# Rows backwards as the last scan direction, and outputs and inputs of a joint stage handed out to the same end

## The chip, the cores and the metric

The kernel runs on one core of one Trainium2 chip. A core has a matrix engine (TensorE, PE), a vector engine (VectorE, DVE), an activation engine (ScalarE, ACT), a general-purpose engine (GpSimd, POOL) and a sync engine (SyncE, SP) that here issues every transfer. The engines run side by side, each in the order of its own instructions, and wait for one another by semaphores. The metric is the time of one execution on the device, in microseconds (us); less is better.

## The reference

Four images of 64 x 64 positions and 96 channels go through four layers. The first two are selective scans in four directions, the last two are attention without a softmax, followed by a feed-forward network with quantised numbers. What matters here is a scan layer (`DI` = 192 inner channels, 16 states):

```python
xz = einsum('bhwc,ec->bhwe', group_norm(x), in_proj_w)      # 96 -> 2 x 192
xc, z = split(xz)
xc = silu(depthwise_conv3x3(xc) + conv_b)
xs = [xc by rows, xc by columns, rows backwards, columns backwards]   # k = 0, 1, 2, 3
dts, B, C = split(einsum('bkdl,kcd->bkcl', xs, x_proj_weight))
delta = softplus(einsum('bkrl,kdr->bkdl', dts, dt_projs_weight) + bias)
# for each direction, channel and state, along the 4096 positions l:
h[l] = exp(delta[l] * A) * h[l-1] + delta[l] * xs[l] * B[l]
ys[l] = sum over states of h[l] * C[l]  + D * xs[l]
y = ys of the four directions, each put back to its positions, added
y = layernorm(y) * silu(z)
x = x + einsum('bhwd,cd->bhwc', y, out_proj_w)
```

The four directions are added, so the order in which they are computed is free.

## The kernel before, in words

**Units.** A unit is one scan layer on one pair of images; there are four, in the order (layer 0, pair 0), (layer 0, pair 1), (layer 1, pair 0), (layer 1, pair 1). The 192 channels of two images are 384 rows: three tiles of 128, of which the third (j = 2) holds the last 64 channels of both images. Before a unit's scan stand its inputs (`scan_inputs`): normalisation, projection, convolution, silu; after it its outputs (`scan_outputs`): layer norm, gate, projection, residual. After the last unit come the token layers 2 and 3 (`token_layers`).

**The scan (`PairScan`, lines 370-733).** `steps` (line 374) lists 48 steps: four directions k, four chunks ci of 1024 positions, three tiles j. In each step the 16 states are taken two at a time: ScalarE makes the exponentials, ScalarE with TensorE, or TensorE with VectorE, make the input terms, VectorE runs the recurrence (line 715), GpSimd multiplies by C (line 730), and TensorE transposes and adds up into `yp`. At the end of a step `finish_sum` (line 661) copies the sum to `ysum` and stores it to `y` in memory. A step of k > 0 first loads what is there already (`load_kept`, line 654) and adds onto it. `chunk_of` (line 385) says which positions a step has: odd k run by columns, k >= 2 backwards, so that k = 2 ends with the first rows and k = 3 with the first columns of all rows. By columns a tile's store is twice as many transfers as by rows (`places`, line 640). All compute instructions of the scan stay in the program's order. At the first step of a direction the weights of the next are loaded (line 687).

**Joint stages (`between_scans`, lines 142-154).** Between two scans the outputs of the unit before and the inputs of the next one are issued together. Both are generators. `scan_outputs` stops after each of its 16 groups of 256 positions (`for g`, line 282). `scan_inputs` stops 20 times: four times in the projections of each image (lines 242-254, two chunks of 512 positions to a stop), and twice for each of six rounds of convolution (lines 258-264): one block as nine products on TensorE (`conv_product`), one or more rows of `next(beginnings)`, which projects and discretises the first step of the next scan, and one block as nine multiply-adds on VectorE (`conv_chain`, lines 203 and 205). The handing out is

```python
            for _ in outs:
                for _ in range(2):
                    next(ins, None)
```

The program's order gives priorities; a scheduler at build time puts the instructions of each engine into their final order from them.

**A group of outputs.** Loads `zt`, `xr`, `ys` (lines 285-298); statistics on VectorE (303, 304); the reciprocal root on GpSimd (line 81); `shift` on VectorE (307); the norm on ScalarE (311); six transposes into `pt` on TensorE (319); scale and bias on ScalarE (321); the gate on VectorE (328); the products `po` on TensorE (335 in layer 0; 345 to 348 in layer 1); the residual `xo` (337 on VectorE in layer 0, 350 on ScalarE in layer 1); the store. In layer 0 each group also takes statistics for the next group norm (line 117), which are put together after the last group (line 358). The tiles come from the pool `c2` (line 276), in two sets, or three in the stage of the last unit.

**Memory.** A scan's tiles and those of the stages around it share the same memory one after the other: a stage's first instruction on a tile waits for whatever last used that place. In the last stage, `token_layers` drives the outputs of the last unit together with the token layers of the first two images (lines 924-936).

Of the kernel before, what the change touches and what calls it, by code (L numbers as in the profile page):

```python
# [27 lines left out]
L = HW * HW  # L28
# [6 lines left out]
K = 4  # L35
# [4 lines left out]
T = 1024  # L40
# [5 lines left out]
NT = L // 128  # L46
# [29 lines left out]
def rstd_of(nc, pool, var, shape, tag, half):  # L76

    ve = pool.tile(shape, F32, name=f"{tag}_ve")
    nc.vector.tensor_scalar(ve, var, EPS, None, ALU.add)  # L79
    rs = pool.tile(shape, F32, name=f"{tag}_rs")  # L80
    nc.gpsimd.tensor_tensor(rs, ve, half, ALU.pow)  # L81
    return rs
# [59 lines left out]
def between_scans(tc, cst, ident, half, pn, u, before, scan, after):  # L142


    with ExitStack() as stage:
        ins = scan_inputs(tc, stage, cst, ident, half, pn, u, scan, *after)
        if before is not None:
            pp = stage.enter_context(tc.tile_pool(name="c_ps", bufs=2, space=PSUM))
            outs = scan_outputs(tc, stage, cst, ident, half, pn, *before, pp)
            for _ in outs:  # L150
                for _ in range(2):
                    next(ins, None)
        for _ in ins:
            pass


def scan_inputs(tc, stage, cst, ident, half, pn, u, scan, layer, pr):


# [112 lines left out]
def scan_outputs(tc, stage, cst, ident, half, pn, layer, pr, pp, turned="pt", summed="po"):  # L272

    nc = tc.nc
    par, zg, x_src, x_dst, y = layer.par, layer.zg[pr], layer.x_src, layer.x_dst, layer.y[pr]
    p2 = stage.enter_context(tc.tile_pool(name="c2", bufs=3 if layer.last and pr else 2))
    if not layer.last:
        norms = [GroupNorm(p2, pn, f"gn{2 * pr + i}", NT // 2) for i in range(2)]
    wo = p2.tile([128, 3, C], F32, name="wo", bufs=1)
    nc.sync.dma_start(out=wo, in_=layer.w["wo"].rearrange("s p c -> p s c"))  # L280

    for g in range(NT // 2):
        at = 256 * g
        zt = p2.tile([128, 3, 256], F32, name="zt")
        nc.sync.dma_start(out=zt, in_=zg[:, :, at : at + 256].rearrange("j p t -> p j t"))
        xr = p2.tile([C, 2, 256], F32, name="xr")
        nc.sync.dma_start(out=xr, in_=x_src[2 * pr : 2 * pr + 2, :, at : at + 256].rearrange("i c t -> c i t"))


        ys = p2.tile([128, 2, 3 * 128], F32, name="ys")  # L290
        for i, to, of in (
            (0, slice(0, DI), slice(0, DI)),
            (1, slice(DI, 256), slice(D0, DI)),
            (1, slice(256, 384), slice(0, D0)),
        ):
            nc.sync.dma_start(
                out=ys[:, :, to], in_=y[i, at : at + 256, of].rearrange("(t p) d -> p t d", p=128)
            )
        stats = p2.tile([128, 2, 2, 6], F32, name="ystats")
        mv = p2.tile([128, 2, 2, 2], F32, name="ymv")  # L300
        for t in range(2):
            for i in range(2):
                nc.vector.bn_stats(stats[:, t, i], ys[:, t, DI * i : DI * i + DI])
                nc.vector.bn_aggr(mv[:, t, i], stats[:, t, i])
        rs = rstd_of(nc, p2, mv[:, :, :, 1], [128, 2, 2], "ln", half[:, 0:4].rearrange("p (t i) -> p t i", i=2))
        shift = p2.tile([128, 2, 2], F32, name="shift")
        nc.vector.scalar_tensor_tensor(shift, mv[:, :, :, 0], -1.0, rs, ALU.mult, ALU.mult)
        for t in range(2):
            for i in range(2):
                cols = slice(DI * i, DI * i + DI)  # L310
                nc.scalar.activation(
                    ys[:, t, cols], ys[:, t, cols], AF.Identity, bias=shift[:, t, i : i + 1], scale=rs[:, t, i : i + 1]
                )

        gt = p2.tile([128, 3, 2, 128], F32, name="gt")
        for t in range(2):
            pt = pp.tile([128, 3, 128], F32, name="pt", tag=turned)
            for j, first in enumerate((0, 256, 128)):
                nc.tensor.transpose(pt[:, j], ys[:, t, first : first + 128], ident)
            for s, js in ((0, slice(0, 2)), (1, slice(2, 3))):  # L320
                nc.scalar.activation(
                    gt[:, js, t],
                    pt[:, js],
                    AF.Identity,
                    bias=par[:, s, P_NB : P_NB + 1],
                    scale=par[:, s, P_NW : P_NW + 1],
                )
        nc.vector.tensor_tensor(gt, gt, zt.rearrange("p j (t q) -> p j t q", q=128), ALU.mult)
        bufs = 1 if summed == "po" else None
        if not layer.last:  # L330
            po = pp.tile([C, 2, 256], F32, name="po", tag=summed, bufs=bufs)
            for i in range(2):
                for q, j in ((0, i), (1 + i, 2)):
                    v = gt[:, j].rearrange("p t q -> p (t q)")
                    nc.tensor.matmul(po[:, i], wo[:, q], v, start=(q == 0), stop=(q > 0))
            xo = p2.tile([C, 2, 256], F32, name="xo")
            nc.vector.tensor_tensor(xo, xr, po, ALU.add)
            nc.sync.dma_start(out=x_dst[2 * pr : 2 * pr + 2, :, at : at + 256].rearrange("i c t -> c i t"), in_=xo)
            for i in range(2):
                norms[i].take(nc, xo[:, i])  # L340
        else:
            po = pp.tile([128, 2, 2, C], F32, name="po", tag=summed, bufs=bufs)
            for t in range(2):
                for i in range(2):
                    nc.tensor.matmul(po[:, t, i], gt[:, i, t], wo[:, 0], start=True, stop=False)
                    nc.tensor.matmul(po[:, t, i], gt[:, 2, t], wo[:, 1 + i], start=False, stop=False)
                    v = xr[:, i, 128 * t : 128 * t + 128]
                    nc.tensor.matmul(po[:, t, i], v, ident[:C, :C], start=False, stop=True, is_transpose=True)
            xo = p2.tile([128, 2, 2, C], F32, name="xo")
            nc.scalar.copy(xo, po)  # L350
            for i in range(2):
                there = (2 * pr + i) * L + at
                nc.sync.dma_start(
                    out=x_dst[there : there + 256, :].rearrange("(t p) c -> p t c", p=128), in_=xo[:, :, i]
                )
        yield
    if not layer.last:
        layer.after.norms[pr] += [norm.norm(nc, pp, turned, cst, half) for norm in norms]


def load_weights(nc, pk, w, k):

    wx = pk.tile([128, 3, NC], F32, name="wx")
    nc.sync.dma_start(out=wx, in_=w["wx"][k])
    wdt = pk.tile([NC, 3, 128], F32, name="wdt")
    nc.sync.dma_start(out=wdt, in_=w["wdt"][k])
    return wx, wdt


class PairScan:  # L370

    steps = [(k, ci, j) for k in range(K) for ci in range(L // T) for j in range(3)]

    def __init__(self, tc, pk, pq, pd, cst, ident, u, layer, pr):
        self.tc, self.pk, self.pq, self.pd = tc, pk, pq, pd
# [109 lines left out]
    def scan(self, stage, nc):  # L487
        tc, ident, steps, projected, made = self.tc, self.ident, self.steps, self.projected, self.made
        amat, dsum, w, y, weights, chunk_of = self.amat, self.dsum, self.w, self.y, self.weights, self.chunk_of
        sel = self.cst["sel"]  # L490
        pk = self.pk
        p2 = stage.enter_context(tc.tile_pool(name="b_2", bufs=2))
# [4 lines left out]
        def begin_project(k, ci):  # L497
            return self.project(nc, nc.gpsimd, odd if ci % 2 else self.pq, pm, "m1", k, ci)

        def begin_discretise(at):  # L500
            return self.discretise(nc, nc.gpsimd, odd if at % 2 else self.pq, pm, ("m0", "m1"), at)
# [175 lines left out]
        def begun(pieces):  # L677
            return [next(pieces), pieces]

        for g, (at, n0) in enumerate(groups):  # L680
            k, ci, j = steps[at]
            rev, first, final = k >= 2, ci == 0, ci == L // T - 1
            if n0 == 0:
                if first and j == 0:
                    last = [pk.tile([128, NS], F32, name=f"last{i}", tag=f"last{i}") for i in range(3)]
                    if k + 1 < K:
                        weights[k + 1] = load_weights(nc, pk, w, k + 1)
                if j == 0:
                    projecting = begun(begin_project(*steps[at + 3][:2])) if at + 3 < len(steps) else []
                discretising = begun(begin_discretise(at + 1)) if at + 1 < len(steps) else []  # L690
# [403 lines left out]
```

## Time and profile before

| what | us |
|---|---|
| median of 3 runs (lowest, highest) | 10643.59 (10634.33, 10654.25) |
| profiled execution: its own time | 10644.94 |
| its span, first to last instruction | 10643.2 |
| first inputs, until the first scan instruction | 158.3 |
| four scans (158.3 to 2456.9; 2682.0 to 4979.4; 5201.0 to 7495.3; 7718.5 to 10010.0) | 2298.6, 2297.4, 2294.3, 2291.5 |
| three joint stages | 225.1, 221.6, 223.2 |
| last outputs and token layers | 633.1 |

Busy over the span: VectorE 90%, GpSimd 85%, ScalarE 82%, TensorE 76%. A share of the whole span is a mean over scans, joint stages and token layers, which have different limits; so the joint stages are read in stretches of their own below. Such a line gives the stretch, its length, then the busy time of TensorE, its weight loads, VectorE, ScalarE and GpSimd (with counts), the TensorE clock as a share of full speed, the busy share of the DMA engines and the GB/s they moved. A line of waits reads: engine, tile and line that waited, what it waited for, then us in total, times, longest.

### The profile page before, as it was taken

What the parts mean: (1) busy time and instruction counts of PE and PEld (TensorE: products, weight loads), DVE (VectorE), ACT (ScalarE), POOL (GpSimd) and SP (SyncE); (2) the same over time, 40 slices, a digit from 0 to 9 for tenths busy, and PEclk for the clock granted to TensorE, in tenths of its full rate; (3) what the DMA queues carried; (4) which work ended last, traced back from release to release, by engine and by line L of the source; (5) the groups of instructions that cost most, each with busy time, mean ns of one, the idle gap of its engine ahead of it and who ended that gap; (6) DMA issues with size and microseconds to landing.
All of it is one profiled execution on the core that took longest, in us unless ns stands there. A gap on an engine that the chain in (4) does not pass through costs nothing. (4 is left out here: it accounts for less than half of the span.)

```text
span 10643.2 us, 142480 instructions
## 1 busy us (share of the span) xinstructions
PE 8055.8 (76%) x47648; PEld 5971.9 (56%) x47648; DVE 9608.1 (90%) x6922; ACT 8760.2 (82%) x18779; POOL 9008.7 (85%) x5298
## 2 busy tenths in 40 slices
PE   7777777777777777777877777777777777777666
PEld 4555555554555555555455555555455555555554
DVE  8999999997899999998899999999699999999755
ACT  6888888885888888887688888888598888888666
POOL 3999999993899999997499999999299999999745
PEclk9888899988888898988888988998888889899877
DMA  4677777775667777777467777777566777777710
GB/s 154 208 211 215 216 222 218 219 213 158 196 210 216 217 220 220 219 214 210 149 209 211 220 219 218 220 219 217 143 209 211 213 220 219 220 217 219 199 35 25
DMA packets 905175, 2120.41 MB, mean 199 GB/s; under 512 B 330583, under 2 KB 640153, under 8 KB 706713
## 3 DMA queue, kind: packets, MB, share of 16 engines
q1 hardware_dynamic: 904440, 2111.30, 68.3%
q8 instruction: 378, 6.19, 0.2%
q14 instruction: 357, 2.92, 0.1%
HBM read 1949.56 MB, written 161.48 MB: 198 GB/s over the span
## 5 line engine op out<-in xcount | busy, mean ns | idle before, releaser
L71 POOL TENSOR_TENSOR h<-h,cb 128x1024 f32<-128x1024 f32 x3072 | 7191.2, 2364 | 234.4 <-issue 58.6
L71 DVE TENSOR_TENSOR_SCAN h<-da,last,bp 128x1024 f32<-128x1024 f32 x2064 | 4736.8, 2335 | 147.1 <-PE bp L71 23.8
L71 ACT ACTIVATE x<-dut,bt 128x128 f32<-128x128 f32 x12288 | 3494.8, 370 | 1.5 <-PE bp L71 1.1
L71 PE MATMUL yp<-ident,h 128*128 128x128 f32 x24576 | 3370.2, 297 | 9.8 <-POOL h L71 9.8
L71 PEld LDWEIGHTS yp<-ident,h 128*128 128x128 f32 x24576 | 3197.1, 157 | 125.7 <-issue 75.5
L71 ACT ACTIVATE da<-delta,amat 128x1024 f32<-128x1024 f32 x2752 | 3060.2, 1138 | 96.0 <-DVE h L71 94.9
L71 PE MATMUL bp<-ident,x 128*128 128x128 f32 x10240 | 1679.2, 316 | 1282.1 <-DVE h L71 923.7
L71 PEld LDWEIGHTS bp<-ident,x 128*128 128x128 f32 x10240 | 1362.6, 162 | 1840.7 <-ACT x L71 1026.7
L71 DVE TENSOR_TENSOR bp<-du,bp 128x1024 f32<-128x1024 f32 x1472 | 1780.1, 1213 | 266.0 <-PE bp L71 264.4
L71 DVE TENSOR_TENSOR_SCAN h<-da,bp 128x1024 f32<-128x1024 f32 x688 | 1537.7, 2274 | 52.7 <-ACT da L71 11.4
L71 PE MATMUL bp<-bparts,sel 96*128 96x512 bf16 x2944 | 918.8, 398 | 760.4 <-DVE h L71 741.2
L71 PEld LDWEIGHTS <-sel 96*128 96x128 bf16 x2944 | 226.8, 100 | 1554.8 <-DVE h L71 1043.7
L71 ACT ACTIVATE bp<-delta,amat 128x1024 f32<-128x1024 f32 x320 | 358.1, 1119 | 528.3 <-DVE h L71 526.3
L71 POOL TENSOR_TENSOR dbu<-du,bb 128x1024 f32<-128x1024 f32 x320 | 754.6, 2358 | 0.0
L71 DVE TENSOR_TENSOR_SCAN h<-bp,last,dbu 128x1024 f32<-128x1024 f32 x240 | 558.9, 2329 | 10.4 <-POOL dbu L71 7.1
L81 POOL TENSOR_TENSOR ln_rs<-ln_ve,half 128x4 f32<-128x4 f32 x64 | 82.4, 1288 | 567.2 <-DVE ln_ve L79 442.0
L71 PE MATMUL xps<-u,wx 128*76 128x512 f32 x720 | 532.0, 824 | 0.0
L71 ACT ACT_TABLE_LOAD x380 | 487.5, 1283 | 34.6 <-DVE gn_norm L138 22.4
L71 POOL COPY last<-h 128x2 f32<-128x2 f32 x1152 | 215.8, 187 | 351.0 <-DVE h L71 349.1
L71 POOL TENSOR_TENSOR du<-delta,u 128x1024 f32<-128x1024 f32 x188 | 496.2, 2639 | 0.0
L71 ACT COPY ysum<-yp 128x1024 f32<-128x1024 f32 x192 | 194.4, 1012 | 300.3 <-PE yp L71 300.3
L71 PE MATMUL dps<-cdt,wdt 12*128 12x512 f32 x752 | 435.0, 658 | 0.0
(159 smaller groups left out, 6328.0 us busy)
## 6 DMA issues: line engine op xcount, KB each, us to landing
cb<-crow SPq DMA_DIRECT2D x1024, 1024.0 KB
cb<-crow SPq DMA_DIRECT2D x1024, 512.0 KB
bb<-crow SPq DMA_DIRECT2D x384, 256.0 KB
bb<-crow SPq DMA_DIRECT2D x128, 512.0 KB
y<-ysum SPq DMA_DIRECT2D x192, 256.0 KB
kept<-y SPq DMA_DIRECT2D x160, 256.0 KB
y<-ysum SPq DMA_DIRECT2D x64, 512.0 KB
zt<-zg SPq DMA_DIRECT2D x64, 384.0 KB
```

The costliest lines, as they stand in the source:

```text
L71: return self.tc.keep_in_program_order(getattr(self.engine, op)(*args, **kwargs))
L81: nc.gpsimd.tensor_tensor(rs, ve, half, ALU.pow)
```

## The change

Four edits. The directions are taken in the order 0, 1, 3, 2, so that rows backwards come last and the first rows are finished last; the loading of the next direction's weights follows that order. The outputs go from the last group of rows to the first. In a joint stage an output is followed by one stop of the inputs, every fourth output by two, instead of two each. The pool of the outputs has three sets in every stage.

```diff
@@ between_scans
-            for _ in outs:
-                for _ in range(2):
+            for g, _ in enumerate(outs):
+                for _ in range(2 if g % 4 == 3 else 1):
                     next(ins, None)
@@ scan_outputs
-    p2 = stage.enter_context(tc.tile_pool(name="c2", bufs=3 if layer.last and pr else 2))
+    p2 = stage.enter_context(tc.tile_pool(name="c2", bufs=3))
...
-    for g in range(NT // 2):
+    for g in reversed(range(NT // 2)):
@@ PairScan
-    steps = [(k, ci, j) for k in range(K) for ci in range(L // T) for j in range(3)]
+    ways = (0, 1, 3, 2)
+
+    steps = [(k, ci, j) for k in (0, 1, 3, 2) for ci in range(L // T) for j in range(3)]
@@ PairScan.scan
-                    if k + 1 < K:
-                        weights[k + 1] = load_weights(nc, pk, w, k + 1)
+                    for after in self.ways[self.ways.index(k) + 1 :][:1]:
+                        weights[after] = load_weights(nc, pk, w, after)
```

## The prediction

> **What bounds the kernel now.** I read the page's 40 slices first, then the busy times by stretch, the waits of two stretches, the timeline of the tail of a joint stage, and the start of the last stage. In the slices
>
> ```profile
> DVE  8999999997899999998899999999699999999755
> PEclk9888899988888898988888988998888889899877
> ```
>
> VectorE is at 90% or more except in three dips and the token layers at the end. The four scans fill 158-2457, 2682-4979, 5201-7495 and 7718-10010 us: 9182 us in all, 574 us a direction. The dips are the three joint stages of 225.1, 221.6 and 223.2 us (the outputs of the last pair with the inputs of the next); 633 us of token layers end it. The first joint stage in stretches (busy us of each engine, TensorE's clock, share of the DMA engines, GB/s):
>
> ```profile
> 2487.00:2537.00 50.00, 43.98 (x122) 20.85 (x121) 46.02 (x72) 40.59 (x78) 2.94 (x2) 0.97 0.76 229
> 2537.00:2617.00 80.00, 75.15 (x229) 36.22 (x229) 73.48 (x132) 35.88 (x71) 12.31 (x7) 1.00 0.29 84
> 2617.00:2632.00 15.00, 14.72 (x53) 7.60 (x51) 5.26 (x15) 10.00 (x18) 1.01 (x1) 1.00 0.36 105
> 2632.00:2682.00 50.00, 29.49 (x88) 17.83 (x88) 24.49 (x80) 20.04 (x44) 5.12 (x6) 0.67 0.38 115
> ```
>
> For 130 us VectorE is 92% busy (119.5 us) and TensorE 92% (119.1 us): full. The inputs' last instruction (the copy of `dut`) ends at 2632. Then six outputs are left and nothing else: VectorE falls to 49%, the clock to 0.67. The waits of that tail form a ring,
>
> ```profile
> DVE xo L337 <- PE po L335: 13.1, 5, 3.7
> PEld po L335 <- DVE gt L328: 10.3, 4, 2.8
> ACT ys L311 <- DVE shift L307: 9.8, 4, 3.9
> ACT gt L321 <- PE pt L319: 8.9, 3, 3.9
> ```
>
> each engine waiting for another about 2.5 us per group, with no engine full. The timeline of one group there shows the price of the low clock:
>
> ```profile
> 2662.49 3.65 PE L335 MATMUL po<-gt,wo 128*96 128x256 f32 x8 [2.53 <-DVE gt L328]
> ```
>
> Eight products take 3.65 us; where the clock is 1.00, they start 0.216 us apart, 1.73 us for eight. A group takes 6.7 us here.
>
> [...]Here the last stores of `y` are issued by 2464.4 and the constants that wait for them (line 172) start at 2466.7, 2.3 us later.
>
> **The change part by part.**
>
> *Directions 0, 1, 3, 2.* The same 48 steps per unit with the same instructions; only their order changes. The stores and loads of `y` keep their distance: a step's old sum is loaded one and a quarter steps, 60 us, after the latest store of those rows, whichever direction follows. The first unit's directions last 576, 580, 570 and 573 us, so swapping the last two costs nothing by itself. I take 0 for the scans, with -6 to +6 us as bound: the four scans of before, with equal code, differ by up to 7 us (2298.6 to 2291.5).
>
> *Rows last.* Its last tile is stored in two transfers per unit where the transposed direction needs four. The four took 2.68 us to issue, so 1.3 us less, ahead of everything that waits for the landing: 1.3 us in each joint stage and at the start of the token layers, where SP's queue then issues weights and `zt` for 15 us without a break.
>
> *Outputs from the last rows.* Their first rows are stored early, but that frees nothing: in the built order of the changed kernel the first load of the outputs (`wo`, and `zt`, `xr`, `ys` behind it on SP) still waits for the last `y` stores and for the last products of the scan, because its memory was the scan's. So 0 us for the order itself. What moves is smaller: the first three `xn` loads now stand ahead of the last stores, so inputs may begin some us sooner. I count nothing for that; bound 0 to -4 us a stage.
>
> *Handing out.* There are 20 stops in the inputs. Before, two pass per output: ten outputs are woven in, six are left. Now 16 outputs pass 12x1 + 4x2 = 20. The built order of TensorE shows it: before, the last product of the inputs (`dups`) is followed by six outputs' transposes and products; after, by none, only by the four small products of the group norm. No instruction is added or removed in the stage, so its sums stay: VectorE 157.5 us, 149.2 of it after 2487.
>
> *Three buffers.* A third set of tiles in these stages; loads wait for the release one group later. In the tail, `ystats` waited for `ys` 6.6 us in two waits; that wait goes with the tail anyway. I count 0.
>
> The stage after: from 2487, 149.2 us of VectorE work at a busy share s, 1.3 us earlier, then what cannot be woven. That is two last groups in which VectorE is half idle, as in the tail (about 3.2 us each, 6.4), and some 4 us of idle time in the group norm's chain of small steps after the last output. For s I take 0.89, not the 0.92 of now: an output has eight hand-offs between engines and VectorE executes in order, so more outputs bring more waits ahead of the convolution's sums queued behind them; and the projections, whose stretch has the DMA at 0.76, now share it with six or seven outputs rather than four. 149.2/0.89 = 167.6; first scan at 2487 + 167.6 - 1.3 + 6.4 + 4 = 2663.7 instead of 2682.0: 18.3 us less. The second stage has the same sums: 18.3.
>
> In the third, layer 1, VectorE has only 134.9 us and TensorE bounds: 124.0 busy of 130 us in 7526-7656. Its work from 7526 is 46.4 + 77.5 + 12.6 and six groups at full clock, each 6 x 0.109 + 8 x 0.112 + 4 x 0.087 = 1.9 us, so 11.4: 147.9 us. At 0.89: 166.2; first scan at 7526 + 166.2 - 1.3 + 10.4 = 7701.3 instead of 7718.5: 17.2 us less.
>
> *Token layers.* The stage already had three buffers and its interleaving isn't touched; its built order is the same except for which rows come first. 1.3 us less from the two stores.
>
> Sum: 18.3 + 18.3 + 17.2 + 1.3 = 55.1 us. The profiled execution took 10644.9 us, 1.7 around its span of 10643.2; less 55.1 it is 10589.8. The median of runs is 1.35 us under it: **10588 us**, 0.5% faster.
>
> **Rivals.**
>
> *A part of it (chance 0.13).* The projections become DMA-bound. An output moves 384 + 192 + 384 + 192 KB = 1.15 MB. From 2487 to 2537 the DMA engines moved 229 GB/s at 0.76, so about 300 GB/s is their limit here. Two and a half outputs more and one more prefetch are about 4 MB, 13 us at that rate; with 24% free in 65 us nearly all would fit, which speaks against it. If half of the transfers block the queue of SP, which issues all loads in order, 7 to 10 us come back per stage: total 25 us, 10619 us.
>
> *Nothing (0.06).* The idle time moves from the tail into the woven part. VectorE's idle time in the tail is 25.5 us, 4.2 per output. If each of the six moved outputs brings the same 4.2 us inside, the stage stays: 10642 us. For this s must fall to 0.80. Against it: ten outputs already run inside at 0.92, and the waits of that stretch on VectorE are small (`shift` for POOL's power: 8.4 us for nine).
>
> *Slower (0.07).* The same mechanism above that point. VectorE's queue holds an output's step that waits for TensorE, and the convolution's sums behind it are late; then the silu, the projection of the first chunk, and its softplus, product and transposes, which now stand at the very end with no cover. At 6 us per moved output it is 36 - 25.5 = 10.5 us more per stage, 32 us in all: 10675 us. It decides from s below 0.80.
>
> **Chances and range.** The first case has 0.74, with its own range from s = 0.95 (149.2/0.95 = 157.1, 29 us a stage, with the scans' bound: 10552 us) to s = 0.86 (12 us a stage, 10607 us). I call anything within 0.2% (21 us, about what this measurement can tell from no change) the same. Faster: the first case and half of the partial one, 0.81. Same 0.12, slower 0.07. The range 10556 to 10630 takes in the partial case and leaves out no change and slower.
>
> **What would show it.** Joint stages of 203 to 208 us from the last scan to the first; VectorE's share near 0.9 up to the last 15 us; the clock at 1.00 there instead of 0.67; `po` products eight in about 1.8 us all through; no output after `dups`. Scans of 2290 to 2300 us each. Wrong would be: a stage still over 220 us, with `u` (lines 203-205) waiting behind `gt`, `xo` or `shift`; `xn` or `ys` waiting for DMA in the first 70 us; or scans longer by more than 6 us each, which would mean that the order of directions isn't free.

## The result

The changed kernel takes 10599.66 us (median of six runs, 10598.68 to 10605.4), the kernel before beside it 10644.94 us (median of six): a ratio of 0.9959, with a 95% interval from 0.9947 to 0.9971. It is faster by 0.4%, about 45 us. The prediction was 10588 us with a range from 10556 to 10630.

The profiled execution took 10598.68 us, with a span of 10596.9 us; before it was 10643.2. By stage, in us:

| stage | before | after | difference |
|---|---|---|---|
| first inputs | 158.3 | 157.4 | -0.9 |
| joint stages 1, 2, 3 | 225.1, 221.6, 223.2 | 205.0, 205.3, 203.4 | -20.1, -16.3, -19.8 |
| scans 1, 2, 3, 4 | 2298.6, 2297.4, 2294.3, 2291.5 | 2293.9, 2294.0, 2293.1, 2305.5 | -4.7, -3.4, -1.2, +14.0 |
| last outputs and token layers | 633.1 | 639.2 | +6.1 |
| span | 10643.2 | 10596.9 | -46.3 |

The joint stages give 56.2 us; the last scan and the token layers take 20 of it back, the first inputs and the first three scans give 10 more.

### The profile page after: what moved, and what is told of

Read it like the earlier page. It is cut to its first block, busy times and chain, and to the rows that moved or that the text cites. A ratio compares the mean times of both kernels' runs of the same rounds, so it can differ in the third digit from the quotient of the medians.

```text
span 10596.9 us, 142441 instructions
## 1 busy us (share of the span) xinstructions
PE 8040.9 (76%) x47648; PEld 5960.5 (56%) x47648; DVE 9612.6 (91%) x6922; ACT 8759.0 (83%) x18779; POOL 9017.1 (85%) x5298
## 4 chain that ended last, share of the span: by engine, by line
ACT 34%; issue 18%; PE 18%; DVE 17%; POOL 10%; DMA 2%; SPq 0%; DVEq 0%; POOLq 0%; ACTq 0%
ACT x L71 14%; ACT da L71 12%; DVE h L71 10%; PE yp L71 7%; POOL h L71 6%; PE bp L71 5%; DVE bp L71 4%; ACT bp L71 2%; PE xps L71 1%; DMA cb<-crow 1%; PE dps L71 1%; ACT L71 1%; POOL dbu L71 1%; PE dups L71 1%; DVE u L205 1%
```

## The profile after

The first joint stage of the changed kernel (2451.3 to 2656.3 us) in stretches, with the columns of the prediction's lines: the stretch, its length, the busy time of TensorE, its weight loads, VectorE, ScalarE and GpSimd, TensorE's clock, share of the DMA engines, GB/s.

```profile
2451.30:2482.00 30.70, 15.15 (x55) 8.64 (x56) 14.43 (x42) 13.11 (x26) 12.36 (x26) 0.72 0.71 185
2482.00:2532.00 50.00, 44.75 (x131) 22.03 (x129) 45.96 (x82) 41.52 (x83) 5.65 (x3) 0.93 0.76 225
2532.00:2612.00 80.00, 72.44 (x206) 34.88 (x207) 72.44 (x146) 37.16 (x75) 12.29 (x8) 0.91 0.42 120
2612.00:2627.00 15.00, 12.91 (x54) 7.20 (x53) 13.16 (x30) 10.51 (x20) 4.24 (x2) 1.00 0.31 87
2627.00:2656.30 29.30, 24.47 (x90) 13.02 (x88) 13.14 (x36) 13.83 (x23) 2.10 (x3) 0.96 0.20 66
```

VectorE is 91% busy for 145 us; the 50 us of tail with 49% and a clock of 0.67 are gone, and 29 us are left in which VectorE is at 45%, while TensorE, at a clock of 0.96, is busy for 84%. What ends the stage is seen in TensorE's own timeline there (start, duration, instruction, count):

```profile
2640.98 1.89 PE L336 MATMUL po<-gt,wo 128*96 128x256 f32 x8
...
2643.74 1.94 PE L336 MATMUL po<-gt,wo 128*96 128x256 f32 x8
2645.52 3.60 PE L189 MATMUL cps<-img,diag 128*128 128x512 f32 x8
2648.95 1.04 PE L481 MATMUL dups<-ident,du 128*128 128x128 f32 x8
2649.82 0.25 PE L126 MATMUL gm<-mv,group 96*96 96x1 f32 x2
```

The products of the last two outputs take 1.9 us instead of 3.65, and the inputs' last product (`dups`) now stands behind them: both parts end together. Ahead of that the clock is lower than before, 0.93 and 0.91 in the stretches of 50 and 80 us, where it was 0.97 and 1.00. The waits from 2612 us on (who waited for what: us in total, times, longest):

```profile
DVE du L474 <- ACT delta L472: 6.1, 1, 6.1
ACT ys L312 <- DVE shift L308: 4.4, 2, 3.2
PEld po L336 <- DVE gt L329: 3.4, 2, 2.8
...
DVE xo L338 <- PE po L336: 2.0, 2, 1.3
```

Of the ring of the tail (13.1, 10.3, 9.8 and 8.9 us in its four lines) a few single waits remain. The longest of VectorE's is now `du`: the product for the first step of the next scan waits 6.1 us for ScalarE's `delta`, with no other VectorE work to lie beside it. It waited before too, 4.4 us, ahead of the tail.

## The experiments

**The change in parts.** Four kernels, each the kernel before with some of the four edits. The first has the handing out alone:

```diff
-            for _ in outs:
-                for _ in range(2):
+            for g, _ in enumerate(outs):
+                for _ in range(2 if g % 4 == 3 else 1):
```

> The kernel before with the handing out alone (one stop, every fourth output two). Theory A, the six outputs behind the inputs are the whole cost: joint stages of 205 to 210 us, 40 to 50 us less in all, ratio 0.9955. Rival B, three buffers carry it, because with two sets the woven outputs wait for their tiles: stages near 220 us, 10 us less in all, ratio 0.999.

The second has the third set of tiles alone:

```diff
-    p2 = stage.enter_context(tc.tile_pool(name="c2", bufs=3 if layer.last and pr else 2))
+    p2 = stage.enter_context(tc.tile_pool(name="c2", bufs=3))
```

> The kernel before with three buffers in every joint stage alone. Theory A: the ring of the last six outputs stays, stages within 2 us of before, ratio 1.000. Rival B: the tail's groups follow each other in less than 6.7 us and the stages shrink by 10 us or more each, ratio 0.997.

The third has the new order of directions and the outputs from the last rows, nothing else (`ways`, `reversed(range(NT // 2))`):

> The kernel before with the order of directions 0, 1, 3, 2 and outputs from the last rows alone. Theory A: each stage 1.3 us shorter for two stores less, scans unchanged in sum, 5 us less in all, ratio 0.9995, no more than the scatter. Rival C, the order of directions lengthens the last scan (2305 us in the changed kernel, 2291 before): a last scan near 2305 us again and a ratio of 1.000 to 1.001.

The fourth has handing out and three sets, with directions and outputs in the old order:

> The changed kernel with the old order of directions and of outputs. Theory A: joint stages of 205 us as in the changed kernel, ratio 0.996. Rival C: the last scan is back at 2291 us and the token layers at 633 us, so that it gains 56 us, ratio 0.9947, and beats the changed kernel.

| kernel | median, us | ratio to before (95%) | joint stages 1, 2, 3 | sum |
|---|---|---|---|---|
| before | 10648.05 | | 225.1, 221.6, 223.2 | 669.9 |
| handing out | 10610.72 | 0.9967 (0.9956 to 0.9978) | 210.8, 208.3, 206.8 | 625.9 |
| three sets | 10614.71 | 0.9967 (0.9955 to 0.9979) | 212.6, 210.2, 217.7 | 640.5 |
| directions and output order | 10636.91 | 0.9993 (0.9987 to 1.0) | 222.3, 221.6, 226.3 | 670.2 |
| handing out, three sets | 10591.09 | 0.9949 (0.9937 to 0.9962) | 207.9, 207.3, 207.2 | 622.4 |
| all (the changed kernel) | 10599.66 | 0.9959 (0.9947 to 0.9971) | 205.0, 205.3, 203.4 | 613.7 |

The stages are those of one profiled execution each, and they scatter: the kernel before and one further down (computed tiles with a third set), which take the same time, differ by 4.3, 2.3 and 1.7 us in their stages.

Handing out gives 44.0 us in the stages, and is the cause of most of the gain. The surprise is the third set of tiles: alone it is worth 29.4 us, with six outputs still in the tail; after the handing out only 3.5 more. The two edits go after the same idle time. The order of directions and outputs does nothing alone (+0.3 us in the sum); on top of the other two the stages are 8.7 us shorter, but the time of the whole is not: the intervals of the last two rows overlap.

**Which tiles wanted a third set.** The loaded tiles in one kernel, those that an output computes in another, both on the kernel before:

```diff
-        zt = p2.tile([128, 3, 256], F32, name="zt")
+        zt = p2.tile([128, 3, 256], F32, name="zt", bufs=3)
...
-        xr = p2.tile([C, 2, 256], F32, name="xr")
+        xr = p2.tile([C, 2, 256], F32, name="xr", bufs=3)
...
-        ys = p2.tile([128, 2, 3 * 128], F32, name="ys")
+        ys = p2.tile([128, 2, 3 * 128], F32, name="ys", bufs=3)
```

> The kernel before, with a third buffer for the three loaded tiles of an output alone (zt, xr, ys; the last stage has them already). Three buffers for all tiles took 29.5 us from the three joint stages (670.0 to 640.5). Theory A, the loads were late: with two buffers an output's ys can be fetched only once the output two before it has let go of its ys, and the statistics queued on VectorE wait for it; then this kernel keeps most of the gain, stages of 640 to 648 us in all, time about 10615. Theory B, the work tiles held the outputs back (a statistic, gt or xo of an output may not be written until two outputs before it is through): then stages of 662 to 670 us, time about 10640.

The other has `bufs=3` for `ystats`, `ymv`, `shift`, `gt` and `xo`.

> The kernel before, with a third buffer for the tiles that an output computes alone (ystats, ymv, shift, gt, xo), and two for zt, xr and ys. Theory A (loads late): stages of 662 to 670 us in all, as before. Theory B (work tiles): 640 to 648 us. If both kernels keep a half, about 655 us each, the two waits stand in a row and either one holds an output back.

Loaded tiles: 10617.59 us, ratio 0.998 (0.9972 to 0.9988), stages 218.1, 214.9 and 220.2, sum 653.2. Computed tiles: 10645.41 us, ratio 1.0005 (0.9996 to 1.0014), stages 220.8, 223.9 and 224.9, sum 669.6. The loads bring 16.7 us of the 29.4, the computed tiles alone 0.3, so 12.4 us are missing that come only where both have three sets. In SyncE's queue, which issues every load and store in order, the waits that a third set is meant for can be seen. In the first joint stage of the kernel before,

```profile
SPq L296 <- PE pt L319: 43.7, 11, 17.1
SPq L338 <- DVE xo L337: 28.8, 11, 6.5
```

line 296, the load of `ys`, stands 43.7 us, eleven times, until TensorE has transposed the `ys` that still occupies the memory; every later load is behind it, and in the longest of these waits, the 17.1 us from 2553.0 on, SyncE issues nothing. With three sets for the loaded tiles alone it is

```profile
SPq L338 <- DVE xo L337: 33.4, 10, 7.6
SPq L296 <- PE pt L319: 33.2, 7, 16.6
```

and in the changed kernel (where line 297 is that load)

```profile
SPq L339 <- DVE xo L338: 26.0, 9, 12.4
SPq L297 <- PE pt L320: 24.5, 5, 18.1
```

Most of this lies ahead of the tail: in the tail itself it is 5.6 us before and 1.1 with three sets of loads. What VectorE's statistics wait for the data of `ys` in the tail stays as it was, in the kernel before and then with three sets of loads:

```profile
DVE ystats L303 <- DMA ys<-y: 6.6, 2, 5.8
DVE ystats L303 <- DMA ys<-y: 6.8, 2, 5.7
```

In the first stage an output in the tail takes 6.9 us from `dut` on in the kernel before and 5.7 with three sets of loads. The difference is made by the first four of the six, whose residuals `xo` start 3.4 to 3.8 us apart instead of 4.5 to 9.2; the last two come 8.0 and 6.9 us later, as slowly as before (6.7 and 6.8). This fits loads that have run ahead and are then used up; no run tried it apart.

For the missing 12.4 us there are two explanations. Either an output also waits for its computed tiles once the loads are free, or the third set of these only takes memory and so moves the tiles behind it: with three sets of all, the first three `xn` loads of the first two stages start 4.4 us before the scan ends, with three sets of loads alone 13.2 us or more after it. So the last kernel has three sets of loads and an unused tile in place of the third set of the others:

```diff
-    p2 = stage.enter_context(tc.tile_pool(name="c2", bufs=3 if layer.last and pr else 2))
+    p2 = stage.enter_context(tc.tile_pool(name="c2", bufs=3 if layer.last and pr else 2)); pad = None if layer.last and pr else p2.tile([128, 1328], F32, name="pad", bufs=1)
```

> The kernel before, with a third buffer for the three loaded tiles (zt, xr, ys) and, in place of the third set of the computed tiles, an unused tile of 5312 bytes a partition. It uses no more than memory: the tiles behind it lie elsewhere, and in the built order SyncE's loads and stores come as in the kernel with three sets for all, the first three xn loads among them, which stand ahead of the last scan's end in the first two joint stages. Three sets of loads alone gave 653.2 us in the three joint stages, three sets of all 640.5. Theory A, the computed tiles held the outputs back: stages as with three sets of loads alone, 650 to 656 us. Theory B, placement: the early xn loads and the order that follows from them give the difference, and this kernel has it too: 638 to 644 us, about 10614 us in all, with the gain of 4 to 6 us in the first two stages and less in the third.

10617.7 us, ratio 0.9972 (0.9961 to 0.9984), stages 209.6, 209.5 and 217.8, sum 636.9, even 3.6 us under three sets of all. The computed tiles' third set does nothing by itself: the memory that it takes, and with it the place of the tiles behind, makes the difference. In the time of the whole the two kernels with three sets of loads are not told apart (0.998 and 0.9972, with intervals that overlap); the stages show it. The `xn` loads are early in the first two stages, and these are 8.5 and 5.4 us shorter than with the loads' sets alone, the third, where `xn` is as late as ever (13.1 us), only 2.4. In the first stage `dut` ends 168.5 us in, instead of 175.8. Whether the early loads themselves bring this, or something else that moved with the memory, was not tried apart.

**The clock in the tail.** Three more products per output for the last six outputs of the two layer-0 stages, into `po`, which the real products then overwrite; the kernel before otherwise:

```diff
+            if g > 9:
+                for i in (0, 1, 0):
+                    nc.tensor.matmul(po[:, i], wo[:, 0], ys[:, 0, 0:256], start=True, stop=True)
```

> The kernel before, where each of the last six outputs of the two layer-0 stages has three more products into its own sum (overwritten by the real ones), placed ahead of the four real ones where TensorE waits for the gate. They do no work; they keep the array busy. The third stage is left alone. Theory D, the low clock is a good part of the tail: the four real products take 1.8 us instead of 3.65, and the two stages shrink by up to 10 us each, to 213 us. Rival E, the hand-offs between the engines are the tail and the clock only goes along with them: the stages stay at 222 to 225 us, or grow by the 8 us that the extra products take.

One run: 10637.84 us beside 10640.33. The clock comes up: eight products of a late output, as in this line of its timeline, take 1.9 or 1.97 us in all six, instead of 3.6 to 3.7 in five of them.

```profile
2652.05 1.97 PE L338 MATMUL po<-gt,wo 128*96 128x256 f32 x8 [1.18 <-DVE gt L328]
```

TensorE's half-clock time (the time for which the record has its clock at 0.5) in the first stage falls from 53.6 to 32.3 us. But that stage is only 7.1 us shorter, the second 2.3 (218.0 and 219.3), with the cost of the added products in it; handing out took 14.3 and 13.3 us from the same two stages. So the low clock is at most a part of the price of the tail, and 2.3 us is within the scatter of a stage: the groups still wait for one another, as the bracket says of `gt`.

**More tail.** Two kernels with three sets and the new order, in which the inputs run out sooner: three stops per output (nine outputs left over), and all 20 after the first output (15 left over).

```diff
-                for _ in range(2 if g % 4 == 3 else 1):
+                for _ in range(3):
```

> The changed kernel with three stops of the inputs per output: seven outputs woven in, nine behind the inputs, three buffers. Theory A at the price that six trailing outputs had with three buffers (213.5 less 207.5 us, 1.0 us per output): stages of 213 to 216 us. Rival F, with three buffers the trailing outputs cost nothing by themselves: 205 to 208 us.

The other has `range(20)`.

> The changed kernel with all 20 stops after the first output: one output first, then the inputs, then 15 outputs. Theory A: start 17 us, inputs alone 130 us as in the first stage of the kernel, 15 outputs at the 5.5 us that they take in a tail with three buffers, 9 us at the end: stages near 238 us, longer than before the change. At a linear 1.0 us per trailing output they would be 220 us. Rival F: 205 to 210 us.

Stages of 214.9, 217.8 and 223.8 us for nine (10618.37 us, one run); 227.8, 232.4 and 240.9 for fifteen (10684.32 us, one run). Against the 205.0, 205.3 and 203.4 of none: 1.1, 1.4 and 2.3 us per output left over, then 1.5, 1.8 and 2.5. Rival F is out, and the price is not linear. In the kernel with two sets, six outputs left over cost 14.3, 13.3 and 16.4 us (before against handing out alone), 2.2 to 2.7 each. So an output outside the weave costs 1.1 to 2.7 us, depending on sets, layer and number, well under the 4.2 us of VectorE idle time that the tail shows per output: the rest of the idle time comes back inside.

**The start.** The changed kernel with the inputs' weights and their first stop (two chunks) put ahead of the first output:

```diff
+            next(outs)
+            next(ins)
+            next(ins)
             for g, _ in enumerate(outs):
-                for _ in range(2 if g % 4 == 3 else 1):
+                for _ in range(2 if g % 5 == 4 else 1):
```

(with a bare `yield` after the inputs' weights and one after `wo`.)

> The changed kernel with the inputs set up first in each joint stage: the weights of the projection are loaded ahead of the first output's tiles, and the first two chunks are projected ahead of the first output. If the start of a stage (first VectorE instruction on an output 15 us after the scan) is a price that the order of loads sets: stages 2 to 5 us shorter, 200 to 203 us, ratio 0.9945. If the stage is set by the sum of VectorE's work alone: unchanged at 205 us, ratio 0.996.

10591.75 us, ratio 0.9954 (0.994 to 0.9967); stages 206.4, 207.7 and 209.9, not one shorter than with the plain order. But the edit moves the end as well. The inputs are through sooner: `dut` ends 192.1, 192.9 and 198.7 us into the stages, instead of 199.5, 199.8 and 200.9. One output is then left behind them, and from `dut` to the scan it takes 14.4, 14.9 and 11.2 us instead of 5.5, 5.5 and 2.5. So the run does not show that the start is worth nothing; it shows that this way of going about it gains nothing.

**Whose time is the woven part?** The changed kernel with the gate moved from VectorE to GpSimd:

```diff
-        nc.vector.tensor_tensor(gt, gt, zt.rearrange("p j (t q) -> p j t q", q=128), ALU.mult)
+        nc.gpsimd.tensor_tensor(gt, gt, zt.rearrange("p j (t q) -> p j t q", q=128), ALU.mult)
```

> The changed kernel with the product of gt and zt moved from VectorE to GpSimd, in all stages. If VectorE's own work is what the woven part is made of, [...]joint stages of 195 to 200 us instead of 203 to 205. If the hand-offs set the pace, GpSimd's slower product [...]lengthens every output's chain by about 1 us and the stages stay at 203 to 208 us or grow; the token layers show the same at the last six outputs.

In the groups of the first joint stage (busy us, mean ns), the changed kernel has

```profile
L329 DVE TENSOR_TENSOR gt<-gt,zt 128x768 f32<-128x768 f32 x16 | 15.2, 951 | 3.3 <-ACT gt L322 3.3
```

and this one

```profile
L329 POOL TENSOR_TENSOR gt<-gt,zt 128x768 f32<-128x768 f32 x16 | 33.1, 2072 | 75.0 <-ACT gt L322 57.4 <-DMA ys<-y 13.1 <-DMA x<-xo 4.5
```

The gate took 0.95 us on VectorE and 2.07 us on GpSimd. The stages are longer by 14.5, 15.2 and 27.8 us (219.5, 220.5, 231.2), the token stage, where the same outputs run, by 27.7; in all 10677.87 us, ratio 1.0035 (1.0022 to 1.0048). That looks like an answer, but VectorE has not been relieved. The whole first stage, in the changed kernel and in this one (VectorE's busy time is the third of the five):

```profile
2451.30:2656.30 205.00, 169.72 (x530) 85.77 (x530) 159.15 (x332) 116.14 (x225) 36.65 (x41) 0.90 0.51 145
2453.80:2673.30 219.50, 172.84 (x530) 86.08 (x530) 161.89 (x315) 116.84 (x225) 64.60 (x57) 0.90 0.49 135
```

The gate's 15.2 us are gone, and VectorE is busy for 2.7 us more. Its other instructions have become longer: `shift` from 2.6 to 7.4 us in all, the multiply-adds of line 205 from 79.8 to 83.7, the first products of line 203 from 6.3 to 10.8. The timeline shows where:

```profile
2564.87 1.80 POOL L329 TENSOR_TENSOR gt<-gt,zt 128x768 f32<-128x768 f32 x1
2564.93 1.75 DVE L308 SCALAR_TENSOR_TENSOR shift<-ymv,ln_rs 128x4 f32<-128x4 f32 x1 [0.90 <-POOL ln_rs L81]
```

A `shift`, 0.16 us by itself, takes 1.75 us beside GpSimd's product and ends with it. So this run cannot tell whether the woven part is paced by VectorE's work or by the succession of an output's steps: the work stayed, and the chain of each output became 1.12 us longer (17.9 us for 16), with GpSimd's reciprocal roots behind `gt` in its queue as well. Only in the third stage does VectorE's busy time fall, from 134.6 to 130.6 us, and that stage is 27.8 us longer; but there TensorE is the fuller engine (173.5 us of 203.4). (Why the third stage and the token layers lose more was not followed up.)

## Why the prediction was right, and where not

| term, us | predicted | measured | from |
|---|---|---|---|
| handing out, three stages | -49.9 | -44.0 | handing out alone |
| third set of tiles | 0 | -3.5 | with handing out, less handing out alone |
| directions, output order, fewer stores, in the stages | -3.9 | -8.7 | changed kernel, less the one without these |
| token layers (two stores less at their start) | -1.3 | +6.1 | stage table |
| scans and first inputs | 0 | +3.8 | stage table |
| sum | -55.1 | -46.3 | span |

**The handing out: right.** The joint stages were to last 203 to 208 us and last 203.4 to 205.3; the part fell where it was said to, with no output behind `dups` and products of 1.9 us. VectorE is near 0.9 up to the last 29 us, where the last 15 were forecast. By the terms of the working, in the first stage: VectorE work after the first 30 us, 149.2 predicted and 144.7 measured (157.5 and 159.15 in the whole stage, so about 6 us of it moved into the first 30 us); idle time in the woven part, 18.4 (149.2/0.89 less 149.2) and 13.4; idle time at the end, 10.4 and 16.2. So s was 0.91 rather than 0.89, and the end was mis-sized by 6 us: the list there had two groups and the group norm, and forgot the 6.1 us of `du` behind `delta`, though the rival "slower" names that very chain as standing at the end with no cover. These misses offset each other in part.

**What s means: not shown.** The working treats VectorE as a full engine that needs 149.2/s us. The gate's move was to test that and could not, since VectorE's total did not fall. So s is a description of the stretch that it was read from, in which the same outputs and sums are interleaved, and no run shows what sets it.

**The third stage: right by two misses that cancel.** There the working puts TensorE in VectorE's place. The stage of the changed kernel:

```profile
7479.00:7529.00 50.00, 43.57 (x163) 23.24 (x163) 45.05 (x80) 39.15 (x78) 6.15 (x4) 0.90 0.82 222
7529.00:7609.00 80.00, 76.11 (x301) 41.95 (x300) 69.41 (x130) 46.91 (x95) 10.21 (x7) 0.98 0.46 133
7609.00:7637.00 28.00, 27.53 (x129) 16.11 (x128) 7.86 (x28) 17.41 (x36) 3.02 (x3) 1.00 0.34 92
7637.00:7652.20 15.20, 12.46 (x71) 8.30 (x69) 3.38 (x5) 8.65 (x15) 0.00 (x0) 0.97 0.31 103
```

TensorE's work in these four lines is 159.7 us, where 147.9 were counted, at a clock of 0.90 and 0.98 in the first two, where it had been 1.00 before; its share up to the last 15 us is 0.93 instead of 0.89. The length, 173.2 us for 175.3, owes its closeness to luck.

**"Three buffers: I count 0": right in the sum, wrong as a reason.** The text names one wait, 6.6 us of `ystats` for `ys`, and lets it go with the tail. That a third set is worth little holds once the tail is gone (3.5 us are left). But this wait is not the one that a third set of loads removes: it is still 6.8 us there. The text misses that a third set of loads brings the first outputs of a tail closer together, and that a larger pool moves the memory of the inputs' tiles; the two are worth 16.7 and some 12 to 16 us without any handing out.

**Early `xn`: right in size, wrong in origin.** The working puts the earlier `xn` loads down to the order of the outputs. They come with the larger pool, in either order: 4.4 us before the scan's end in the first two stages, against 13.9 and 13.2 us after it with handing out alone. Once the parts are handed out they are worth little: three sets on top of it make these two stages 2.9 and 1.0 us shorter and the third, where the loads are not early, 0.4 longer. In the two stages that it concerns this is within the bound of 0 to -4 us. With six outputs left in the tail the same placement gave 8.5 and 5.4.

**Fewer stores: seen at the start, not in the length.** -1.3 us a stage was counted. In the kernel with the new order alone, the loads of `ys` behind the stores start 10.3 us after the scan instead of 11.1 to 11.2, in all three stages. The stages themselves changed by -2.8, 0.0 and +3.1; on top of the rest by -2.9, -2.0 and -3.8. In the token layers the first outputs start 0.2 us sooner only. What the stores are worth in a stage's length cannot be told from its scatter.

**Scans and token layers: +9.9 us where -1.3 was counted.** The last scan is 14.0 us longer and so looks like a cost of the new order. It isn't: with the same order the last scan takes 2295.8 us in the kernel with directions and output order alone, and 2292.1 to 2298.2 us in those with more tail, the earlier start and the gate on GpSimd; and the kernel with the handing out alone, in the old order, has a last scan of 2308.7. A single direction makes the difference: it takes 584.1 us with TensorE at half clock for 143.8 us, where the same direction (columns backwards) takes 572.6 with 111.8 in the second unit. The same pair, 584.1 and 143.8, is found in the first unit of two other kernels. The token stage, too, goes with its half-clock time: 628.4 us with 266 (directions and output order), 628.7 with 259 (earlier start), 633.1 with 290 (before), 636.0 with 284 (three sets of loads), 628.4 with 263 (the same and the unused tile), 639.2 with 307 (the changed kernel), 641.8 with 318 (three sets of computed tiles). That is a rough relation in seven records, not a cause that was tried: waits may stand behind both, and the tail before, with its ring of waits, is where the clock was at 0.67. The bound of -6 to +6 us for the scans was too narrow for one scan, and held for their sum (+4.7). What these lengths go with is in the last section; why a scan meets one or the other is open.

**The rivals.** DMA-bound projections: in the projections' 50 us the DMA engines moved 225 GB/s at 0.76, against 229 at 0.76, and in the 80 us behind them their share only rose from 0.29 to 0.42. The 300 GB/s of the working are the author's estimate (229/0.76), and no run shows a limit there: in a stretch of the changed kernel's last scan, 8800 to 8815 us, 266 GB/s were moved at a share of 0.73. Idle time moving inside: it does by part (1.1 to 2.7 us an output gained instead of 4.2), never by all.

## What to carry to other kernels

When two pieces of work are woven, hand them out so that both end together, and price the gain by what an item costs outside the weave less what it costs inside, not by the idle time of the tail: here 1.1 to 2.7 us of 4.2. Look at the queue that issues the loads before counting a further buffer at nothing: here one line's loads stood 43.7 us in the first stage for the release of their tile, with all later loads behind them. And a pool's size moves the tiles behind it, which can start other loads sooner or later (here the first `xn` loads, 4.4 us before the scan's end instead of 13.2 us or more after it): a filler tile of the same size tells that apart from the buffers themselves. When one product is moved to another engine to test whether the first is the bound, read the first engine's busy time again: here it lost 15.2 us of work and was busy for 2.7 us more. And when parts are handed out anew, look at the end of the stage too: an edit meant for the start left one output behind.

## What the runs showed of the hardware

TensorE's clock stands at 1.0 or at 0.5 in the records. Of the 384 periods at 0.5 in the changed kernel's record, 383 last a multiple of 3.413 us, most of them one or two (135 and 220); in that of the kernel before it is 391 of 392 (148 and 217). Within each of the fourteen records the periods begin on one grid of 3.413 us, to within 0.02 us, and the grid's offset from the first instruction is different from record to record: 0.14 us in the kernel before, 1.93 in the changed kernel, from 0.14 to 2.56 in all. No run shows what sets it.

Equal scan code took one of a few lengths in these runs, each with its own half-clock time. In the changed kernel columns backwards, third in the new order, takes 573.2, 572.6, 576.5 and 584.1 us in the four units, with 112.4, 111.8, 129.4 and 143.8 us of half clock. In the six kernels with that order it stands 24 times: 572.6 or 572.7 us with 108.5 to 111.9 us of half clock (8 times), 573.1 to 573.3 with 112.3 to 115.9 (7), 576.4 to 576.6 with 129.2 to 129.5 (6), and 584.1 with 143.8 (3). Those three are the only ones in which the direction begins 2.5 us past a line of its record's grid; the other 21 begin within 0.15 us of one. That is a relation in 24 cases and was not tried. Two scans of one kernel differed by up to 15 us (2293.6 and 2308.7, with the handing out alone), and the changes compared here were a few us a stage.

In the first stage the product of `gt` and `zt` (128 x 768, f32) took 0.95 us on VectorE in the changed kernel and 2.07 us on GpSimd in the kernel with the gate there (means of 16). In that stage of the latter, some of VectorE's instructions took longer while GpSimd worked on the product: three of 16 `shift`, 1.76 us instead of 0.16, and ten of the 64 multiply-adds of line 205, 1.70 us on average instead of 1.27. The statistics of `ys` (17 of 64 beside it) did not: 0.35 and 0.34 us. What makes the difference was not tried.
